# Two of seven block products of an expert layer split once more into seven

## The chip, the cores and the metric

The kernel runs on one core of a Trainium2 chip. The metric is the device time of one execution in microseconds (us). TensorE multiplies, VectorE (DVE) and ScalarE (ACT) work element by element, GpSimd (POOL) and SyncE (SP) mostly start transfers. TensorE writes its results into banks of a small memory (PSUM), from which VectorE and ScalarE read.

## The reference, cut to what matters

The layer is a gated cross attention followed by a mixture of experts. All is float32. The part that the change touches is the experts' first layer:

```python
# x: 4096 tokens of 512 features; 8 experts, the best 2 for each token, at most cap = 640 tokens per expert
buf = jnp.zeros((e, cap, d), x.dtype).at[e_flat, posc].add(jnp.where(keep[:, None], xf[tok], 0.0))
h = jax.nn.gelu(jnp.einsum('ecd,edf->ecf', buf, w1) + b1[:, None, :], approximate=False)   # 512 -> 2048
out = jnp.einsum('ecf,efd->ecd', h, w2) + b2[:, None, :]                                   # 2048 -> 512
```

`h` is needed by the second layer in full; the results are then weighted and added to the tokens' rows.

## The kernel before, in words

Attention, the router and the dispatch of tokens come first. The third stage, from 1591 us of the span to its end, takes the eight experts one after the other. Per expert the tokens' rows arrive in 5 tiles of 128 (`xb`), are transposed by TensorE (L2105) and copied to `bT` (features on partitions, 640 tokens along the columns).

**First layer.** `hidden(e, idx)` makes one of eight feature blocks: 256 features (two halves, `lo` and `hi`, of 128) for 640 tokens (two halves of `HC` = 320), summed over 512 features of `bT` (two halves of 256, that is two chunks of 128 each). This product of 2 x 2 by 2 x 2 blocks is done with seven instead of eight block products (Strassen's scheme in Winograd's form). Its operands are the blocks and their sums: `w1_forms` of the weights, made by four VectorE sums for each block (`w1_sums`, L1654 to L1657), and `XS` of the tokens, made once per expert (`x_forms`, L2074 to L2077). Each of the seven products is two matmuls of 320 columns; all matmuls pass through the helper `mm` at L2029. Four results share partial sums: ScalarE copies a finished bank into the next one, and further products are added on top. In the order of TensorE:

- product 0 into bank X; ScalarE copies X to Y (L2210; L2207 where the first expert has it early);
- product 3 into Q; ScalarE copies Q to `p5` (L2213);
- product 4 onto Y; ScalarE copies Y to Z (L2216);
- product 1 onto X, and ScalarE's gelu of it (L2221) gives `lo[:, :HC]`;
- product 5 onto Z; ScalarE copies Z to W (L2223); VectorE adds Z and `p5` (L2224) for `hi[:, HC:]`;
- product 6 onto Y; VectorE adds Y and `p5` (L2226) for `lo[:, HC:]`;
- product 2 onto W for `hi[:, :HC]`.

The last three gelus of a block (`owed`, L2229 to L2231) run among the next block's ScalarE operations. Blocks 0 to 3 use the first half of the weights `w1`, blocks 4 to 7 the second. For blocks 0 to 3 of the first expert, products 0 and 1 were already made by `early_product` while rows came in.

**Second layer.** `plain` (two of seven outer products, by matmuls of 256 columns), `deep` (the other five, `7`, `6`, `5`, `4` and `3`, each split into seven products of 128 columns) and `rest` follow. Their operands are formed by VectorE: `left` (L2244 to L2247), `right` (L2259 to L2262), and the inner sums (L2275 to L2284), which lie in `sets[0]` and `sets[1]`. `coefs` (L2093 to L2096) takes weights and indices out of the rows.

**What sets the order.** The order is written by hand. `dv`, `ac`, `ld` and `mm` chain every operation behind the one before of its kind, so each engine works its queue strictly in the order in which the code calls it; the framework adds the waits between engines that the buffers need. The loop over `idx` calls `hidden` and, after it, hands VectorE what later steps need: `w1_sums` for blocks ahead (blocks 4 to 7 after blocks 1 to 4, the next expert's after 6 and 7), `left`, `right`, and the bias rows:

```python
if more and idx == KQ - 1:
    ld(lambda: load_w1(e + 1, 0))
if 1 <= idx <= 4:
    dv(*w1_sums(e, 1, idx - 1))
if idx in (2, 4, 6):
    dv(left(1, idx - 2, idx), left(3, idx - 2, idx))
```

The row tile buffers `xb` are four; the fifth tile of the next expert is loaded (L2040, SP's queue) once VectorE's `coefs` has read the first, and is transposed after the product `6`.

Of the kernel before, what the change touches and what calls it, by code (L numbers as in the profile page):

```python
# [6 lines left out]
F32 = mybir.dt.float32  # L7
I32 = mybir.dt.int32
AF = mybir.ActivationFunctionType
ALU = mybir.AluOpType  # L10
# [4 lines left out]
P = 128  # L15
# [5 lines left out]
def gated_layer(ctx, tc, x, x_t, ctxt, ctxt_t, ctxt_c, ctxt_r, g_xattn, g_ffn, w_sim, w_sim_r, b_sim, W_qv, W_qv_t, b_qv, b_qv_c, w_router, b_router, w1, b1, w2, b2, out):  # L21
# [6 lines left out]
    nc = tc.nc  # L28
    N, D = x.shape
    L = ctxt.shape[0]  # L30
    E, _, FF = w1.shape
    NT = N // P
    DC = D // P
    NF = FF // P
# [76 lines left out]
    with ExitStack() as s1:  # L111
# [6 lines left out]
        ps_tr = s1.enter_context(tc.tile_pool(name="ps_tr", bufs=2, space=PSUM))  # L118
        tt, ts, stt = nc.vector.tensor_tensor, nc.vector.tensor_scalar, nc.vector.scalar_tensor_tensor
# [193 lines left out]
        left = {}  # L313
# [1306 lines left out]
    KH = FH // P  # L1620
    KQ = KH // 2
    KF = 2 * KQ

    def load_w1(e, h):
        w1_of[e, h] = wpool.tile([P, DC, FH], F32, name=f"w1_{e}_{h}", tag="w1", bufs=2)
        return nc.sync.dma_start(w1_of[e, h], w1[e, :, h * FH : (h + 1) * FH].rearrange("(c p) f -> p c f", p=P))
# [15 lines left out]
    def w1_forms(e, h):  # L1642

        W = w1_of[e, h]
        A11, A12, A21, A22 = (W[:, c : c + 2, f * P * KQ : (f + 1) * P * KQ] for f in (0, 1) for c in (0, 2))
        return A11, A12, A22, w1s[0], w1s[1], A21, w1s[2]

    def w1_sums(e, h, f=None):

        cols = slice(None) if f is None else slice(f * P, (f + 1) * P)  # L1650
        A11, A12, A22, S1, S2, A21, S4 = (a[:, :, cols] for a in w1_forms(e, h))
        tt = nc.vector.tensor_tensor
        return [
            lambda: tt(S1, A21, A22, ALU.add),  # L1654
            lambda: tt(S2, S1, A11, ALU.subtract),
            lambda: tt(A21, A11, A21, ALU.subtract),
            lambda: tt(S4, A12, S2, ALU.subtract),  # L1657
        ]
# [3 lines left out]
    with ExitStack() as s2:  # L1662
# [49 lines left out]
        second = c2.tile([P, E], F32, name="second")  # L1712
# [8 lines left out]
        for n in sizes:  # L1721
            t = STEPS[-1][-1] + 1 if STEPS else 0
# [3 lines left out]
        tt, ts, red = nc.vector.tensor_tensor, nc.vector.tensor_scalar, nc.vector.tensor_reduce  # L1726
# [215 lines left out]
        for g in range(len(STEPS)):  # L1942
# [4 lines left out]
            for i in range(ahead):  # L1947
                mm = tile_mm(s, i)
# [16 lines left out]
            if s.n == 2:  # L1965
                with tc.issue_after(mm.ins):
                    place_prev()
                mm = prev.counted
            if s.next is None:

                s.first = ps_mm.tile([P, 2, 512], F32, name="first", tag="mm")[:, 0, :E]
                with tc.issue_after(mm.ins):
                    mm = nc.tensor.matmul(s.first, ones, s.base[:, 0, :], start=True, stop=True)
            elif g + 2 == len(STEPS):

                cnt = ps_mm.tile([P, 2, 512], F32, name="cnt", tag="mm")[:, 0, :E]
                with tc.issue_after(mm.ins):
                    mm = nc.tensor.matmul(cnt, ones, s.base[:, 0, :], start=True, stop=True)
# [19 lines left out]
    with ExitStack() as s3:  # L1998
# [3 lines left out]
        ps_tr = s3.enter_context(tc.tile_pool(name="ps_tr3", bufs=2, space=PSUM, reuse_waits="tile"))  # L2002
        HC = CAP // 2
        MH = 2 * P
        DH = D // 2
        tt, stt = nc.vector.tensor_tensor, nc.vector.scalar_tensor_tensor
        assert KQ == 4 and NST == 5 and DH == 2 * P and KF == 2 * KQ

        banks = [ps_m.tile([P, 512], F32, name=f"bank3_{i}", tag=f"b{i}") for i in range(6)]
        tail = {}  # L2010

        def chained(eng, *ops):

            for op in ops:
                with tc.issue_after(tail[eng].ins) if eng in tail else ExitStack():
                    tail[eng] = op()
            return tail.get(eng)

        def dv(*ops):
            return chained("dv", *ops)  # L2020

        def ac(*ops):
            return chained("ac", *ops)

        def ld(*ops):
            return chained("ld", *ops)

        def mm(ps, a, b, start, stop):
            return chained("pe", lambda: nc.tensor.matmul(ps, a, b, start=start, stop=stop, skip_group_check=True))  # L2029
# [4 lines left out]
        def rows_in(e, s):  # L2034

            if (e, s) == (0, NST - 1):
                xb_of[e, s] = SX.rearrange("p k t -> p (k t)")[:, :R]
            else:
                xb_of[e, s] = sb.tile([P, R], F32, name=f"xb{e}_{s}", tag="xb", bufs=NST - 1)
            return nc.sync.dma_start(xb_of[e, s], buf_d[e * CAP + s * P : e * CAP + (s + 1) * P, :])  # L2040

        sets = [None, None]
# [7 lines left out]
        hT = cb.tile([P, 2, KF, CAP], F32, name="hT", tag="hT")  # L2050
        bT = cb.tile([P, DC, CAP], F32, name="bT", tag="bT")
        B11, B12, B21, B22 = (bT[:, r : r + 2, c : c + HC] for r in (0, 2) for c in (0, HC))
        XT = cb.tile([P, KF, DH], F32, name="XT", tag="XT")
        flat = XT.rearrange("p k d -> p (k d)")
        xT = [flat[:, i * 2 * HC : (i + 1) * 2 * HC].rearrange("p (k t) -> p k t", k=2) for i in range(3)]
        accs = []
        for i in range(NST):
            a = cb.tile([P, D], F32, name=f"acc{i}", tag=f"acc{i}")
            nc.gpsimd.memset(a, 0.0)
            accs.append(a)  # L2060
        b1_t = cb.tile([P, E * NF], F32, name="b1_t", tag="b1")
# [4 lines left out]
        u2, p7 = (cb.tile([P, 2, DH], F32, name=k, tag=k) for k in ("u2", "p7"))  # L2066
# [42 lines left out]
        early = {}  # L2109
# [78 lines left out]

        stored, owed = [], []

        def hidden(e, idx):

            h, f = divmod(idx, KQ)
            col = e * NF + h * KH + f
            lo, hi = hT[:, 0, idx, :], hT[:, 1, idx, :]
            b_lo, b_hi = b1_t[:, col : col + 1], b1_t[:, col + KQ : col + KQ + 1]
            A = [[a[:, k, f * P : (f + 1) * P] for k in range(2)] for a in w1_forms(e, h)]
            X, Q, Y, Z, W = (banks[i][:, :HC] for i in (0, 1, 2 + idx % 2, 4, 5))
            p5 = p5s[idx % 2]
            there = e == 0 and f in early and h == 0  # L2200

            def product(ps, k, start=False):
                for i in range(2):
                    mm(ps, A[k][i], XS[{2: 6, 6: 2}.get(k, k)][i], start and i == 0, i == 1)

            if there:
                ac(lambda: nc.scalar.copy(Y, early.pop(f)))  # L2207
            else:
                product(X, 0, True)
                ac(lambda: nc.scalar.copy(Y, X))  # L2210
            product(Q, 3, True)
            ac(*owed[:1])
            ac(lambda: nc.scalar.copy(p5, Q))  # L2213
            ac(*owed[1:2])
            product(Y, 4)
            ac(lambda: nc.scalar.copy(Z, Y))  # L2216
            ac(*owed[2:])
            owed.clear()
            if not there:
                product(X, 1)  # L2220
                ac(lambda: nc.scalar.activation(lo[:, :HC], X, AF.Gelu, bias=b_lo))  # L2221
            product(Z, 5)
            ac(lambda: nc.scalar.copy(W, Z))  # L2223
            dv(lambda: tt(hi[:, HC:], Z, p5, ALU.add))  # L2224
            product(Y, 6)
            dv(lambda: tt(lo[:, HC:], Y, p5, ALU.add))  # L2226
            product(W, 2)
            owed.extend([
                lambda: nc.scalar.activation(hi[:, HC:], hi[:, HC:], AF.Gelu, bias=b_hi),  # L2229
                lambda: nc.scalar.activation(lo[:, HC:], lo[:, HC:], AF.Gelu, bias=b_lo),  # L2230
                lambda: nc.scalar.activation(hi[:, :HC], W, AF.Gelu, bias=b_hi),  # L2231
            ])


        lo, hi = hT[:, 0], hT[:, 1]
# [4 lines left out]
        def left(kind, k0, k1):  # L2240

            a11, a21, a12, a22, sx = (a[:, k0:k1, :] for a in (A11, A21, A12, A22, SX))
            return {
                1: lambda: tt(sx, a21, a22, ALU.add),  # L2244
                3: lambda: tt(a21, a11, a21, ALU.subtract),
                2: lambda: tt(a11, sx, a11, ALU.subtract),
                4: lambda: tt(a12, a12, a11, ALU.subtract),  # L2247
            }[kind]
# [73 lines left out]
        for e in range(E):  # L2322
            more = e + 1 < E
# [17 lines left out]
            def add(s, c, src):  # L2341
                return lambda: stt(accs[s][:, c], src, cf[:, s : s + 1], accs[s][:, c], ALU.mult, ALU.add)  # L2342

            (B11w, B12w, B21w, B22w), right, inner = output(e)
            bias = [add(s, slice(None), b2_t) for s in range(NST)]
            for idx in range(2 * KQ):
                if more and idx == 2:
                    ld(*[lambda s=s: rows_in(e + 1, s) for s in range(NST - 1)])
                hidden(e, idx)
                if more and idx == KQ - 1:  # L2350
                    ld(lambda: load_w1(e + 1, 0))
                if 1 <= idx <= 4:
                    dv(*w1_sums(e, 1, idx - 1))
                if idx in (2, 4, 6):
                    dv(left(1, idx - 2, idx), left(3, idx - 2, idx))
                if idx == 3:
                    dv(right(1, 0, 4))
                if idx == 5:
                    dv(right(1, 4, 8), *bias[:2])
                if idx == 6:  # L2360
                    dv(*bias[2:])
                    if more:
                        dv(*w1_sums(e + 1, 0, 0), *w1_sums(e + 1, 0, 1))
                if idx == 7 and more:
                    dv(*w1_sums(e + 1, 0, 2))
# [56 lines left out]
            X, Q, Y, Z, W = deep(f7, 3)  # L2422
# [8 lines left out]
            for m in range(2):  # L2431
                dst = accs[2 + m].rearrange("p (j d) -> p j d", j=2)
# [10 lines left out]
            f4, s4, t4 = inner("4")  # L2443
# [87 lines left out]
```

## Time and profile before

| what | value |
|---|---|
| median of 3 runs | 2563.72 us (2563.48 to 2563.97) |
| profiled execution | 2565.51 us, span 2563.7 us |
| granted TensorE clock | 0.998 |
| TensorE matmul busy | 2543.1 us, 99% of the span |
| VectorE busy | 1844.5 us, 72% |
| ScalarE busy | 693.2 us, 27% |
| one expert, transposes to transposes (1774.98 to 1896.49) | 121.51 us; TensorE busy 121.51, VectorE 83.01, ScalarE 36.39 |

The span runs from the first to the last instruction of the profiled execution. A line of a timeline has the start in us, the length, the engine, the source line, the operation, what is written and read, the count, and in brackets how long the engine stood idle before and what released it. Matmuls overlap, and their ends are modelled.

### The profile page before, as it was taken

How to read it: one execution, taken by the hardware profiler on the slowest of the kernel's cores; microseconds unless marked ns; L12 is line 12 of the kernel's file. 1: busy time of each engine (PE TensorE's matmuls, PEld its weight loads, DVE VectorE, ACT ScalarE, POOL GpSimd, SP SyncE). 2: the span in 40 equal slices, each digit the busy share in tenths (PEclk: the TensorE clock that was granted, in tenths of full speed). 3: DMA queues.
4: the chain of work that ended last, by engine and by line, in shares of the span. 5: the costliest groups of instructions: out<-in, count | busy, mean ns of one | idle time of the engine just before them, and what ended most of it. 6: DMA issues, size and time to landing. Idle time of an engine off the chain costs nothing.

```text
span 2563.7 us, 36624 instructions
## 1 busy us (share of the span) xinstructions
PE 2543.1 (99%) x13964; PEld 2196.9 (86%) x13964; DVE 1844.5 (72%) x3670; ACT 693.2 (27%) x1459; POOL 275.9 (11%) x400
## 2 busy tenths in 40 slices
PE   9999999999999999999999999999999999999999
PEld 7788888998988989989989886787888878787978
DVE  8887965977877868759668666767675858484937
ACT  1112302223123123132230244323233232313140
POOL 0101220001001001000000066010101010101010
PEclk9999999999999999999999999999999999999999
DMA  7568795875976857759758795231314141414120
GB/s 260 197 214 299 270 346 168 288 255 177 315 232 207 284 192 263 258 180 304 244 166 281 274 350 202 83 128 66 132 67 156 46 160 38 161 42 156 50 99 21
DMA packets 198399, 488.99 MB, mean 191 GB/s; under 512 B 22462, under 2 KB 79102, under 8 KB 196176
## 3 DMA queue, kind: packets, MB, share of 16 engines
q1 hardware_dynamic: 151984, 386.37, 44.7%
q0 software_dynamic: 21696, 59.07, 6.4%
q10 hardware_dynamic: 24544, 41.21, 4.4%
q8 instruction: 110, 1.80, 0.3%
q14 instruction: 65, 0.53, 0.1%
HBM read 397.40 MB, written 97.52 MB: 193 GB/s over the span
## 4 chain that ended last, share of the span: by engine, by line
PE 88%; issue 5%; DVE 5%; POOL 1%; DMA 1%; ACT 0%; POOLq 0%; SPq 0%; another core or an unknown queue 0%; DVEq 0%; ACTq 0%
PE bank L2029 31%; PE bank L763 21%; PE bank L986 13%; PE bank L1155 6%; PE bank L1512 5%; PE x1p L1757 3%; PE bank L1256 2%; PE p7d L1512 1%; PE p4d L1512 1%; PE bank L815 1%; PE v L1256 1%; DVE SM L1025 1%; PE bank L992 1%; DVE hqT L1192 1%; PE bps L2105 1%
## 5 line engine op out<-in xcount | busy, mean ns | idle before, releaser
L763 PE MATMUL bank<-Qp,kt 128*128 128x256 f32 x1344 | 305.2, 379 | 0.0
L763 PEld LDWEIGHTS bank<-Qp,kt 128*128 128x128 f32 x1344 | 254.4, 190 | 34.1
L2029 PE MATMUL bank<-w,hT 128*128 128x256 f32 (+1 forms) x1280 | 260.7, 359 | 0.7 <-ACT u L2408 0.7
L2029 PEld LDWEIGHTS bank<-w,hT 128*128 128x128 f32 x1280 | 223.8, 190 | 27.4 <-ACT u L2408 1.1
L763 PE MATMUL bank<-q,kt 128*128 128x256 f32 x1008 | 231.3, 379 | 0.0
L2029 PE MATMUL bank<-bT,w 128*128 128x320 f32 x736 | 218.8, 433 | 2.0 <-ACT bank L2216 1.6
L763 PEld LDWEIGHTS bank<-q,kt 128*128 128x128 f32 x1008 | 191.5, 190 | 26.0
L2224 DVE TENSOR_TENSOR hT<-bank,l 128x320 f32<-128x320 f32 x64 | 31.5, 492 | 253.4 <-ACT bank L2223 253.4
L986 PE MATMUL bank<-dt,vf 128*128 128x128 f32 x1680 | 204.8, 275 | 0.0
L986 PEld LDWEIGHTS bank<-dt,vf 128*128 128x128 f32 x1680 | 196.0, 192 | 0.0
L2029 PEld LDWEIGHTS bank<-bT,w 128*128 128x128 f32 x736 | 139.0, 190 | 60.6 <-ACT bank L2216 3.1
L2029 PE MATMUL bank<-XT,w1s 128*128 128x320 f32 x512 | 148.4, 433 | 0.0
L806 DVE TENSOR_TENSOR M<-M,E_all 128x1024 f32<-128x1024 f32 x80 | 97.8, 1223 | 47.8 <-ACT E_all L723 46.4
L2029 PEld LDWEIGHTS bank<-XT,w1s 128*128 128x128 f32 x512 | 97.2, 190 | 40.6 <-ACT bank L2207 0.4
L2397 POOL DMA_INDIRECT out<-acc,ti x40 | 39.6, 990 | 819.2 <-DVE acc L2342 812.5
L1757 PE MATMUL x1p<-W,q2T 128*128 128x264 f32 x512 | 119.8, 396 | 0.5 <-DVE p1d L1527 0.5
L1757 PEld LDWEIGHTS x1p<-W,q2T 128*128 128x128 f32 x512 | 98.8, 195 | 18.0 <-DVE p1d L1527 0.9
L719 DVE TENSOR_TENSOR E_all<-bank,p5s 128x512 f32<-128x512 f32 x42 | 28.9, 689 | 114.5 <-ACT bank L718 114.5
L893 DVE TENSOR_TENSOR E_all<-E_all,mb 128x1024 f32<-128x1024 f32 x84 | 101.2, 1211 | 10.3 <-ACT mb L868 10.3
L986 PE MATMUL bank<-E_all,vf 128*128 128x128 f32 x828 | 106.5, 275 | 0.0
L894 ACT ACTIVATE E_all<-E_all 128x1024 f32<-128x1024 f32 x84 | 88.8, 1057 | 49.8 <-DVE E_all L893 49.3
L986 PEld LDWEIGHTS bank<-E_all,vf 128*128 128x128 f32 x828 | 99.8, 192 | 0.3
(602 smaller groups left out, 4755.9 us busy)
## 6 DMA issues: line engine op xcount, KB each, us to landing
vf<-vf_d SPq DMA_DIRECT2D x122, 768.0 KB
kt<-kt_d SPq DMA_DIRECT2D x84, 512.0 KB
w<-in_w SPq DMA_DIRECT2D x16, 2048.0 KB
w<-in_w SPq DMA_DIRECT2D x32, 1024.0 KB
kt<-in_ctxt_t SPq DMA_DIRECT2D x84, 384.0 KB
wp<-wt_d SPq DMA_DIRECT2D x56, 520.0 KB
buf_d<-zero SPq DMA_DIRECT2D x80, 129.0 KB
xb<-buf_d SPq DMA_DIRECT2D x39, 258.0 KB
```

The lines of the kernel that those rows point to most:

```text
L763: nc.tensor.matmul(ps[:, jl, :], kts[j][:, KSLOT[p], k, :], B[p][:, k, :], start=start and jl == 0 and k == 0, stop=stop and k == 1, skip_ ...
L806: tt(M, M, e[:, :, h], ALU.max)
L893: live[g]["last"] = tt(e, e, m, ALU.subtract)
L894: live[g]["exp"] = nc.scalar.activation(e, e, AF.Exp)
L986: nc.tensor.matmul(ps, a[:, j, :], rhs[r][:, j, :], start=start and j == 0, stop=j == NP - 1 and (rest is None or add is None), skip_group ...
L1155: nc.tensor.matmul(ps[b], vt[:, j - i * JH, b * P : (b + 1) * P], right(j) if j < NJ else right_c, start=start and j == 0 and b == 0, stop ...
L1256: mm = nc.tensor.matmul(acc[k][:, b, :], a[:, b * P : (b + 1) * P], r, start=start and b == 0, stop=stop, skip_group_check=True,)
L1512: nc.tensor.matmul(ps[m], A[p][:, k, m * P : (m + 1) * P], wt[:, k, :], start=start and k == 0, stop=stop and k == DC - 1, skip_group_chec ...
L1757: mm = nc.tensor.matmul(ps[:, j, :B1], qTs[g][:, c, q * P : (q + 1) * P], W1[:, c, j, :], start=(c == 0), stop=(c == DC - 1))
L2029: return chained("pe", lambda: nc.tensor.matmul(ps, a, b, start=start, stop=stop, skip_group_check=True))
L2224: dv(lambda: tt(hi[:, HC:], Z, p5, ALU.add))
L2397: sc = nc.gpsimd.indirect_dma_start(out=out[:, :], out_offset=rows_of(ti, s), in_=accs[s][:, :], in_offset=None, bounds_check=N - 1, oob_i ...
```

## The change

In blocks 0 to 5, products 6 and 2 are taken out of `hidden`. For each pair of neighbouring blocks (0 and 1, 2 and 3, 4 and 5) the two blocks' products 6 are one product of 256 features, 320 tokens and 256 summed features. It is split into halves in all three and made by seven matmuls of 160 columns; the same for product 2. Such a small set, `parts(e, k, pair, ...)`, is woven into a following block in three steps (`first`, `second`, `third`): set "6" of a pair into block 1, 3 or 5, set "2" into block 2, 4 or 6. Its partial sums X, W and Q lie in one bank of the transposes' pool, Y and Z in another bank. VectorE adds the results onto `hT` (four adds a set), and ScalarE's gelus follow. `deep_x` and `deep_w` form the small sets' operands on VectorE, partly in place, partly in `sets[1]`. Blocks 6 and 7 keep all seven products. The `left` pairs and the load of the next expert's first weights move to later blocks.

```diff
+        def deep_x(k):
+            b, (t1, t2, t4, t3) = x_of[k]
+            b11, b12, b21, b22 = (b[:, c, d : d + HH] for c in range(2) for d in (0, HH))
+            return [
+                lambda: tt(t1, b12, b11, ALU.subtract),
+                lambda: tt(t2, b22, t1, ALU.subtract),
+                lambda: tt(t3, b22, b12, ALU.subtract),
+                lambda: tt(t4, b21, t2, ALU.subtract),
+            ]
+
+        def deep_w(e, k, pair):
...
+            return [
+                lambda: tt(s1, a21, a22, ALU.add),
+                lambda: tt(s2, s1, a11, ALU.subtract),
+                lambda: tt(a21, a11, a21, ALU.subtract),
+                lambda: tt(s4, a12, s2, ALU.subtract),
+            ]
+
+        def parts(e, k, pair, c_bank):
+            XWQ = ps_tr.tile([P, DC, P], F32, name=f"d{e}_{k}{pair}", tag="tr").rearrange("p c t -> p (c t)")
+            X, W, Q = (XWQ[:, i * HH : (i + 1) * HH] for i in range(3))
+            YZ = banks[c_bank][:, : 2 * HH]
+            Y, Z = YZ[:, :HH], YZ[:, HH:]
...
+            def first():
+                mm(X, a11, b11, True, True)
+                ac(lambda: nc.scalar.copy(Y, X))
+                mm(Q, s1, t1, False, True)
+                mm(W, a22, t4, False, True)
+
+            def second():
+                mm(Y, s2, t2, False, True)
+                ac(lambda: nc.scalar.copy(Z, Y))
+                mm(X, a12, b21, False, True)
+
+            def third():
+                mm(Z, s3, t3, False, True)
+                mm(Y, s4, b22, False, True)
+
+            adds = [
+                lambda: tt(dst[:, :, HH:], dst[:, :, HH:], Q.unsqueeze(1).to_broadcast([P, 2, HH]), ALU.add),
+                lambda: tt(dst[:, :, :HH], dst[:, :, :HH], XWQ[:, : 2 * HH].rearrange("p (f t) -> p f t", f=2), ALU.add),
+                lambda: tt(dst[:, 0, HH:], dst[:, 0, HH:], Y, ALU.add),
+                lambda: tt(... Z.unsqueeze(1).to_broadcast([P, 2, HH]), ALU.add),
+            ]
...
         def hidden(e, idx):
...
-            product(Q, 3, True)
-            ac(*owed[:1])
-            ac(lambda: nc.scalar.copy(p5, Q))
-            ac(*owed[1:2])
-            product(Y, 4)
-            ac(lambda: nc.scalar.copy(Z, Y))
-            ac(*owed[2:])
-            owed.clear()
+            if there and idx:
+                ac(lambda: nc.scalar.copy(Y, early.pop(f)))
+                step(0)
+                product(Y, 4)
+                due(1)
+                ac(lambda: nc.scalar.copy(Z, Y))
+                step(1)
+                product(Q, 3, True)
+                ac(lambda: nc.scalar.copy(p5, Q))
+                step(2)
+                due(1)
+            else:
...
+                step(0)
+                due(1)
+                product(Q, 3, True)
+                ac(lambda: nc.scalar.copy(p5, Q))
+                step(1)
...
+                product(Y, 4)
+                ac(lambda: nc.scalar.copy(Z, Y))
+                step(2)
+                due(1)
             if not there:
                 product(X, 1)
                 ac(lambda: nc.scalar.activation(lo[:, :HC], X, AF.Gelu, bias=b_lo))
+            due(len(owed))
+            if split:
+                dv(lambda: tt(lo[:, HC:], Y, p5, ALU.add))
             product(Z, 5)
-            ac(lambda: nc.scalar.copy(W, Z))
+            if part:
+                dv(*part[3])
...
+            ac(lambda: nc.scalar.copy(hi[:, :HC] if split else W, Z))
             dv(lambda: tt(hi[:, HC:], Z, p5, ALU.add))
-            product(Y, 6)
-            dv(lambda: tt(lo[:, HC:], Y, p5, ALU.add))
-            product(W, 2)
+            if not split:
+                product(Y, 6)
+                dv(lambda: tt(lo[:, HC:], Y, p5, ALU.add))
+                product(W, 2)
...
                 hidden(e, idx)
-                if more and idx == KQ - 1:
+                if more and idx == KQ:
                     ld(lambda: load_w1(e + 1, 0))
                 if 1 <= idx <= 4:
                     dv(*w1_sums(e, 1, idx - 1))
-                if idx in (2, 4, 6):
-                    dv(left(1, idx - 2, idx), left(3, idx - 2, idx))
+                if idx == 0:
+                    dv(*deep_w(e, "6", 0), *deep_x("6"), *deep_w(e, "2", 0), *deep_x("2"))
+                if idx == 1:
+                    dv(*deep_w(e, "6", 1), *deep_w(e, "2", 1))
+                if idx == 4:
+                    dv(*deep_w(e, "6", 2), *deep_w(e, "2", 2))
+                if idx in (4, 6, 7):
+                    k = (0, 2, 4)[(4, 6, 7).index(idx)]
+                    dv(left(1, k, k + 2), left(3, k, k + 2))
```

More of the change, by code (lines that the diff above doesn't have):

```diff
@@ L2189, in gated_layer, with w_of @@
         stored, owed = [], []
+        DEEP_IDX = 6
+        HH = HC // 2
+        flat_set = [t.rearrange("p a b -> p (a b)") for t in sets[1]]
+        x_of = {
+            k: (b, [flat_set[i][:, q * HH : (q + 1) * HH] for q in range(3)] + [p7[:, i - 5, :HH]])
+            for k, i, b in (("2", 5, xT[2]), ("6", 6, B22))
+        }
+        def w_of(k, pair):
+            n = 3 * (2 * (pair % 2) + (k == "6"))
+            return [flat_set[2 + (n + q) // 4][:, (n + q) % 4 * P : ((n + q) % 4 + 1) * P] for q in range(3)]
@@ new lines, in deep_x @@
+        def deep_x(k):
[8 more added lines that the diff above has]
+        def deep_w(e, k, pair):
+            a = w1_forms(e, pair // 2)[int(k)]
+            f = pair % 2 * 2 * P
+            a11, a12, a21, a22 = (a[:, c, f + r : f + r + P] for r in (0, P) for c in range(2))
+            s1, s2, s4 = w_of(k, pair)
+            return [
[4 more added lines that the diff above has]
+            ]
@@ new lines, in parts @@
+        def parts(e, k, pair, c_bank):
[3 more added lines that the diff above has]
+            Y, Z = YZ[:, :HH], YZ[:, HH:]
+            a = w1_forms(e, pair // 2)[int(k)]
+            f = pair % 2 * 2 * P
+            a11, a12, s3, a22 = (a[:, c, f + r : f + r + P] for r in (0, P) for c in range(2))
+            s1, s2, s4 = w_of(k, pair)
+            b, (t1, t2, t4, t3) = x_of[k]
+            b11, _, b21, b22 = (b[:, c, d : d + HH] for c in range(2) for d in (0, HH))
+            dst = hT[:, 0, 2 * pair : 2 * pair + 2, HC:] if k == "6" else hT[:, 1, 2 * pair : 2 * pair + 2, :HC]
+            def first():
[14 more added lines that the diff above has]
+                lambda: tt(dst[:, 0, HH:], dst[:, 0, HH:], Y, ALU.add),
+                lambda: tt(
+                    dst[:, 1, :].rearrange("p (d t) -> p d t", d=2), dst[:, 1, :].rearrange("p (d t) -> p d t", d=2),
+                    Z.unsqueeze(1).to_broadcast([P, 2, HH]), ALU.add,
+                ),
+            ]
+            return first, second, third, adds, dst
@@ L2195, in hidden @@
             lo, hi = hT[:, 0, idx, :], hT[:, 1, idx, :]
-            b_lo, b_hi = b1_t[:, col : col + 1], b1_t[:, col + KQ : col + KQ + 1]
+            bias_of = lambda i, n: (lambda c: b1_t[:, c : c + 1])(e * NF + i // KQ * KH + i % KQ + n * KQ)
+            b_lo, b_hi = bias_of(idx, 0), bias_of(idx, 1)
             A = [[a[:, k, f * P : (f + 1) * P] for k in range(2)] for a in w1_forms(e, h)]
@@ L2200, in hidden @@
             there = e == 0 and f in early and h == 0
+            split = idx < DEEP_IDX
+            part = None
+            if 1 <= idx <= DEEP_IDX:
+                k, pair = ("6", idx // 2) if idx % 2 else ("2", idx // 2 - 1)
+                part = parts(e, k, pair, 5 if split else 2 + (idx + 1) % 2)
             def product(ps, k, start=False):
@@ L2204, in product, with step, due @@
                     mm(ps, A[k][i], XS[{2: 6, 6: 2}.get(k, k)][i], start and i == 0, i == 1)
-            if there:
-                ac(lambda: nc.scalar.copy(Y, early.pop(f)))
-            else:
-                product(X, 0, True)
-                ac(lambda: nc.scalar.copy(Y, X))
-            product(Q, 3, True)
-            ac(*owed[:1])
-            ac(lambda: nc.scalar.copy(p5, Q))
-            ac(*owed[1:2])
-            product(Y, 4)
-            ac(lambda: nc.scalar.copy(Z, Y))
-            ac(*owed[2:])
-            owed.clear()
+            def step(i):
+                if part:
+                    part[i]()
+            def due(n):
+                ac(*owed[:n])
+                del owed[:n]
+            if there and idx:
+                ac(lambda: nc.scalar.copy(Y, early.pop(f)))
+                step(0)
[7 more added lines that the diff above has]
+                due(1)
+            else:
+                if there:
+                    ac(lambda: nc.scalar.copy(Y, early.pop(f)))
+                else:
+                    product(X, 0, True)
+                    ac(lambda: nc.scalar.copy(Y, X))
+                step(0)
[3 more added lines that the diff above has]
+                step(1)
+                if not part:
+                    due(1)
+                product(Y, 4)
+                ac(lambda: nc.scalar.copy(Z, Y))
+                step(2)
+                due(1)
             if not there:
@@ L2221, in hidden @@
                 ac(lambda: nc.scalar.activation(lo[:, :HC], X, AF.Gelu, bias=b_lo))
+            due(len(owed))
+            if split:
+                dv(lambda: tt(lo[:, HC:], Y, p5, ALU.add))
             product(Z, 5)
-            ac(lambda: nc.scalar.copy(W, Z))
-            dv(lambda: tt(hi[:, HC:], Z, p5, ALU.add))
-            product(Y, 6)
-            dv(lambda: tt(lo[:, HC:], Y, p5, ALU.add))
-            product(W, 2)
[L2228 to L2232, printed above, removed]
+            if part:
+                dv(*part[3])
+                n = int(k == "2")
+                for i in range(2):
+                    owed.append(
+                        lambda d=part[4][:, i, :], b=bias_of(2 * pair + i, n): nc.scalar.activation(d, d, AF.Gelu, bias=b)
+                    )
+            ac(lambda: nc.scalar.copy(hi[:, :HC] if split else W, Z))
+            dv(lambda: tt(hi[:, HC:], Z, p5, ALU.add))
+            owed.insert(0, lambda: nc.scalar.activation(hi[:, HC:], hi[:, HC:], AF.Gelu, bias=b_hi))
+            if not split:
+                product(Y, 6)
+                dv(lambda: tt(lo[:, HC:], Y, p5, ALU.add))
+                product(W, 2)
+                owed.extend([
+                    lambda: nc.scalar.activation(lo[:, HC:], lo[:, HC:], AF.Gelu, bias=b_lo),
+                    lambda: nc.scalar.activation(hi[:, :HC], W, AF.Gelu, bias=b_hi),
+                ])
         lo, hi = hT[:, 0], hT[:, 1]
```

## The prediction

> **What bounds the kernel now.** I read the page's busy shares, then the chain of waits in order of time, then the timelines of single engines. About 0.2% (5.1 us) is what a measurement of this kernel can tell from no change.
>
> First the busy shares, then seven pieces of the chain (start, length, what) for one expert:
>
> ```profile
> PE 2543.1 (99%) x13964; PEld 2196.9 (86%) x13964; DVE 1844.5 (72%) x3670; ACT 693.2 (27%) x1459; POOL 275.9 (11%) x400
> ```
>
> ```profile
> 1803.55 92.94 PE bank L2029 x456
> 1896.49 0.87 PE bps L2105 x8
> 1897.37 6.98 PE bank L2029 x32
> 1904.35 0.87 PE bps L2105 x8
> 1905.22 19.41 PE bank L2029 x144
> 1924.63 0.44 PE bps L2105 x4
> 1925.07 92.92 PE bank L2029 x456
> ```
>
> TensorE is the chain: one expert follows the next every 121.51 us (1774.98 to 1896.49) without a gap. So a TensorE column saved is time saved, and any new TensorE wait is time lost. The pieces give the pitch of one half of an f32 matmul (each is recorded as two). 32 halves of 256 columns take 6.98: 0.2181 each. 19.41 holds 32 of them and 112 of 128 columns: 0.1110. 92.94 holds 64, 168 and 224 of 320 columns: (92.94 - 13.96 - 18.65)/224 = 0.2693.
>
> **Removed and added on TensorE.** Two products of two blocks were 8 halves of 320 columns, 8 x 0.2693 = 2.154. They become 14 halves of 160. No row has 160; between 128 and 256 columns it is 0.1378 (ends: half of 0.2693 = 0.1347; 160/128 of 0.1110 = 0.1388), so 1.929. Saved: 0.225 per small set (0.21 to 0.27), 6 sets per expert, 8 experts: **-10.8 us** (-10.1 to -12.9).
>
> **Wait A, inside every small set.** `first()` puts X, W and Q of a set into one PSUM bank. It multiplies X, has ScalarE copy X to Y, and goes on to Q. In the built (not run) order of the changed kernel the Q matmul carries a wait on ScalarE, and the next writes to Y and X carry none, so the wait is on that copy. The profile already shows two users of one bank taking turns: VectorE L2224 reads bank Z 0.04 after ScalarE L2223 has read it. Its price, from the first expert, where TensorE has nothing between a product and the copy it needs:
>
> ```profile
> 1594.46 1.34 PE L2029 MATMUL bank<-bT,w 128*128 128x320 f32 x4 [0.55 <-ACT bank L2216]
> ...
> 1600.14 0.41 ACT L2216 COPY bank<-bank 128x320 f32<-128x320 f32 x1 [0.19 <-PE bank L2029]
> ...
> 1600.61 1.34 PE L2029 MATMUL bank<-bT,w 128*128 128x320 f32 x4 [0.50 <-issue]
> ```
>
> Start to start is 6.15 for 20 halves worth 5.39: an uncovered copy costs 0.76. The first four after the wait take 1.34, not 1.24 as later fours do: a restart costs 0.10. So Y's last half ended at 1594.46 + 0.10 + 5.39 = 1599.95, the copy began 0.19 later, and TensorE restarted 0.06 after it. Now the set: count from the end of the big product X0. ScalarE first copies X0 (from 0.19; its next operation follows 0.32 on, at 0.51). X ends at 0.275, is ready at 0.465, is copied from 0.51. A 160-column copy, between the rows of 128 (250 ns) and 320 (410), is 0.277: done 0.79, restart at 0.85, plus 0.10. Without the wait Q would start at 0.275: **0.68 lost** (0.53 if ScalarE does not hold it up and no restart is paid, 0.85 if another operation stands ahead). Everything else of the block is queued behind it. Blocks 2, 3, 4 and 6 pay this: 4 x 8 x 0.68 = **+21.8**. Blocks 1 and 5 wait longer for VectorE, which covers it.
>
> The Trainium skill, "PSUM — Partial Sum Buffer", section on bank collisions, says that semaphores must guard PSUM by bank and quadrant, not by address, a disjoint column range included; that speaks against X and Q in one bank. By addresses alone there would be no wait A and the sum would be 21.8 lower; by the rule it stands. No run shown yet has a TensorE write beside a ScalarE read of other columns.
>
> **Waits B and C, for VectorE's forms.** VectorE's queue at the end of a block:
>
> ```profile
> 1842.75 0.49 DVE L2224 TENSOR_TENSOR hT<-bank,l 128x320 f32<-128x320 f32 x1 [6.46 <-ACT bank L2223]
> 1843.33 0.49 DVE L2226 TENSOR_TENSOR hT<-bank,l 128x320 f32<-128x320 f32 x1
> 1843.74 0.41 DVE L1654 TENSOR_TENSOR w1s<-w 128x256 f32<-128x256 f32 x1
> 1844.19 0.42 DVE L1655 TENSOR_TENSOR w1s<-w1s,w 128x256 f32<-128x256 f32 x1
> 1844.53 0.42 DVE L1656 TENSOR_TENSOR w<-w 128x256 f32<-128x256 f32 x1
> 1844.87 0.42 DVE L1657 TENSOR_TENSOR w1s<-w,w1s 128x256 f32<-128x256 f32 x1
> ```
>
> An add of 320 columns holds VectorE 0.41; 256 columns hold it 0.34, or 0.45 where the next needs its result. Durations 416 ns (256) and 683 (512) give 1.04 ns a column, so 128 columns hold it 0.20 (0.31 dependent, 0.28 to the result) and 160 columns 0.24 (0.345, 0.317).
>
> B: block 0 now ends with product Z, five products after its start, and the `hi` add waits for Z, then for ScalarE's copy of that bank: E + 0.19 + 0.45 = E + 0.64 (E: TensorE's end of block 0). Only then does the queue reach `deep_w`, `deep_x` of set "6": s1 starts at E + 1.05, t1 at 1.97, ready 2.29; t4 ready at 3.11. TensorE wants s1, t1 at E + 1.077 + 0.275 = 1.35 and gets them at 2.35: 1.00 + 0.10. Then W needs t4: TensorE is free at 2.73, t4 seen at 3.17: 0.44 + 0.10. Together 1.65.
>
> C: block 5 wants s1 of pair 2, which stands after block 4: `hi` add at E + 0.67, its 0.41, four `w1_sums` 1.46, s1 from 2.54, seen at 2.88 instead of 1.35: 1.53 + 0.10 = 1.63. In both, the block's products queue behind. The other sets are formed at least a block ahead. B and C: 8 x 3.28 = **+26.2** (1.3 to 2.1 each: 20.8 to 33.6).
>
> **Wait D, the rows of the last tile.** VectorE runs without a gap from 1888.55 to 1921.2 and then frees the buffer for the load that feeds the transposes at 1924.5:
>
> ```profile
> 1921.25 0.34 SPq L2040 DMA_DIRECT2D xb<-buf_d  x1
> ...
> 1924.47 0.60 PE L2105 MATMUL bps<-ident,xb 128*128 128x128 f32 x4
> ...
> 2290.01 0.63 PE L2105 MATMUL bps<-ident,xb 128*128 128x128 f32 x4 [0.88 <-DMA xb<-buf_d]
> ```
>
> That load's traffic ends about 2.4 after its issue in six experts; in the seventh it took 4.1 and TensorE did wait (last line). Moving the `left` pairs (from after blocks 2, 4, 6 to after 4, 6, 7) puts one more pair, 1.44, into this run. Counted from the end of the last block (1896.49 - 6.98 = 1889.51), the issue moves from 31.74 to 33.18, the rows are seen near 35.7, and TensorE wants them at 34.96: 0.7 + 0.10, seven times: **+5.6** (0 to 9, if the run starts earlier or VectorE comes late to it).
>
> **Hidden at no cost.** VectorE's added work, 24 operations of 0.20, 8 of 0.24 and 6 times 1.46 of adds (three of 0.41, one of 0.24), is 15.5 us per expert, beside 38.5 idle (83.0 of 121.5 busy); where it is not hidden it shows as B, C, D. The four adds of a set end before the next block's ScalarE copy needs their bank (about 0.5 before the block ends, and the copy comes 1.5 after), so ScalarE does not wait for them. ScalarE itself gets 12 small copies per expert and is 27% busy. The load of the next expert's first weights is issued one block later, some 8 us: now issued at 1859.5, its traffic is over by 1868 and VectorE first reads it at 1884.7, so 17 are spare; the other half, behind it in SP's queue, is issued near 1890 in any case. If that cover went, VectorE's wait would add to D.
>
> **First expert.** For its blocks 1 to 3 the change puts a product between the copy of Y and its use, so three of its 0.76 waits go (-2.3). But no X0 runs ahead of their sets: B begins 1.08 sooner and costs that more, and in A ScalarE still has two copies ahead (free at 0.86 instead of 0.51), 0.35 more in two blocks. Together **-0.5** (-2 to +1).
>
> **Sum.** -10.8 + 21.8 + 26.2 + 5.6 - 0.5 = +42.3. The profiled execution took 2565.51 with a span of 2563.7; the median of the runs is 2563.72, and the sum is set on that: 2606. All low ends together: +23; all high: +61.
>
> **Rivals.**
> 1. The saving arrives and the waits hide (faster): the copy and the forms land before TensorE asks, 2553. It decides only if an expert's new waits stay under 10.8/8 = 1.35 us; B alone is 1.65 by rows. Chance 0.03, with 0.02 for a balance within 5 us.
> 2. Wait A is cheap (another write lets Q pass early): 2606 - 21.8 = 2584. Against: the wait in the built order. Chance 0.07. That the change does not make its small sets at all is excluded by that order, which has them.
> 3. VectorE falls behind: by my count it has only 0.15 us to spare before block 7's `hi` add. If 2 us more pile up, D grows by 2 x 7 = 14: 2620. For it: the gapless run of 32 us; against: gaps after 1921. Chance 0.13.
> 4. My case, 2606: 0.75.
>
> The range 2590 to 2620 leaves out the faster case, most of rival 2 and the top of rival 3. Slower by over 0.2%: 0.95.
>
> **What would show it.** TensorE idle of 0.5 to 0.7 released by the new ScalarE copy in four blocks per expert; about 1.5 by VectorE in blocks 1 and 5; an expert's period near 121.5 - 1.35 + 6.0 + 0.8 = 127.0; transposes released by the load. A period under 121, or no idle before Q, proves me wrong; DVE-released idle in the second layer would be rival 3.

## The result, and the profile after

| | before | changed |
|---|---|---|
| median of 5 runs | 2563.48 us (2561.88 to 2563.97) | 2609.74 us (2609.28 to 2610.49) |
| profiled execution, its span | 2565.51, 2563.7 us | 2609.41, 2607.4 us |
| granted TensorE clock | 0.998 | 0.999 |
| one expert, transposes to transposes | 121.51 us | 127.12 to 127.30 us |

The changed kernel is slower: ratio 1.0180, 95% interval 1.0168 to 1.0192. The forecast was 2606 us within 2590 to 2620.

The busy shares of the changed kernel, from the page:

```profile
PE 2544.9 (98%) x14252; PEld 2215.0 (85%) x14252; DVE 1975.6 (76%) x4118; ACT 711.5 (27%) x1555; POOL 275.8 (11%) x400
```

TensorE's busy time has hardly moved (2543.1 before), though columns were saved: at every wait the record of the last matmul runs past its pitch, and the first one after it takes longer (0.16 and 0.11 us at the wait below). The share says little here; the new waits have to be read directly. This is who TensorE waited for in the third stage (engine, line, releaser: us in total, times, longest):

```profile
PE d L2029 <- ACT bank L2244: 13.2, 28, 1.1
PE d L2029 <- DVE l L2222: 11.6, 8, 1.5
PE d L2029 <- ACT hT L2341: 6.6, 7, 0.9
PE bps L2105 <- DMA xb<-buf_d: 5.6, 7, 0.9
PE d L2029 <- DVE l L2209: 2.0, 1, 2.0
PE d L2029 <- DVE l L2212: 1.8, 8, 0.2
PE d L2029 <- ACT bank L2313: 1.3, 3, 0.4
PE d L2029 <- issue: 0.4, 1, 0.4
```

`d` is the bank with X, W and Q of a small set. L2244 is ScalarE's copy of X: wait A. It should come 32 times, in four blocks of eight experts; the other four are the last two lines, where the records name the copy of the big product ahead of it (L2313), or nothing. L2222 is the first operation of `deep_w` (s1): wait C, once per expert. L2209 and L2212 are the first and last of `deep_x` (t1, t4): wait B, in two steps. The line with L2341 is also B: the Q matmul of block 1 waits for ScalarE and VectorE together, and a gelu that stood behind the copy ended last by the records (experiment 1 settles the name). The transposes waited for the load of rows in seven experts: D. Every wait that the prediction named is there, and none that it did not name is over 0.7 us in all.

Wait A in block 2 of one expert, from the timeline:

```profile
1856.06 0.43 PE L2029 MATMUL d<-XT,w 128*128 128x160 f32 x2
1856.26 0.41 ACT L2313 COPY bank<-bank 128x320 f32<-128x320 f32 x1 [0.65 <-PE bank L2029]
...
1856.58 0.28 ACT L2244 COPY bank<-d 128x160 f32<-128x160 f32 x1
...
1856.92 0.54 PE L2029 MATMUL d<-l,l 128*128 128x160 f32 x2 [0.42 <-ACT bank L2244]
```

X is multiplied at 1856.06. ScalarE, still in the copy of the big product (L2313), takes X at 1856.58, and Q starts 0.06 after that copy, at 1856.92. The bracket says 0.42, but the loss is larger. X is recorded as 0.43 long, where two halves at their pitch take 0.27 (0.135 each in experiment 6's chain), so 0.16 without work stands as busy; and the restart costs 0.11 (0.54 for two halves instead of 0.43).

Wait B, from the chain in order of time, at the end of block 0:

```profile
1846.22 0.43 ACT hT L2339
...
1846.67 0.49 DVE hT L2340
1847.17 0.21 DVE l L2222
...
1848.10 0.24 DVE l L2209
...
1848.92 0.25 DVE l L2212
1849.17 0.04 issue
1849.21 0.54 PE d L2029 x2
```

The chain leaves TensorE: ScalarE's copy of Z, the `hi` add (L2340), then `deep_w` and `deep_x` in queue order, and only after t4 does the W matmul start. Q had started in between, on t1 (L2209); its row in the timeline names the gelu instead:

```profile
1848.47 0.51 PE L2029 MATMUL d<-l,l 128*128 128x160 f32 x2 [0.95 <-ACT hT L2341]
```

Wait C, the same view in block 5: the four `w1_sums` (L1654 to L1657) lie between the `hi` add and s1.

```profile
1879.57 0.49 DVE hT L2340
1880.06 0.34 DVE w1s L1654
...
1881.19 0.34 DVE w1s L1657
1881.53 0.21 DVE l L2222
1881.74 0.14 issue
```

Wait D, the load and the transposes that need it (SP's queue and TensorE on the timelines):

```profile
1811.71 0.34 SPq L2040 DMA_DIRECT2D xb<-buf_d  x1
...
1814.42 0.63 PE L2105 MATMUL bps<-ident,xb 128*128 128x128 f32 x4 [0.74 <-DMA xb<-buf_d]
```

From the end of that expert's last block (1785.54 - 6.98 = 1778.56) the issue comes at 33.15; 33.18 was forecast. The transposes start at 35.86, where they were wanted at 34.96.

### The profile page after: what moved, and what is told of

Its sections match the earlier page's. It is cut to its first block, busy times and chain, and to the rows that moved or that the text cites. A ratio compares the mean times of both kernels' runs of the same rounds, so it can differ in the third digit from the quotient of the medians.

```text
span 2607.4 us, 37846 instructions
## 1 busy us (share of the span) xinstructions
PE 2544.9 (98%) x14252; PEld 2215.0 (85%) x14252; DVE 1975.6 (76%) x4118; ACT 711.5 (27%) x1555; POOL 275.8 (11%) x400
## 3 DMA queue, kind: packets, MB, share of 16 engines
q1 hardware_dynamic: 151984, 386.37, 43.9%
## 4 chain that ended last, share of the span: by engine, by line
PE 86%; issue 6%; DVE 5%; DMA 1%; POOL 1%; ACT 1%; POOLq 0%; SPq 0%; another core or an unknown queue 0%; DVEq 0%; ACTq 0%
PE bank L2029 28%; PE bank L763 20%; PE bank L986 12%; PE bank L1155 6%; PE bank L1512 5%; PE x1p L1757 3%; PE bank L1256 2%; PE d L2029 2%; PE p7d L1512 1%; PE p4d L1512 1%; PE bank L815 1%; PE v L1256 1%; DMA xb<-buf_d 1%; POOL buf_d L1906 1%; PE bps L2105 1%
## 5 line engine op out<-in xcount | busy, mean ns | idle before, releaser
L2029 PE MATMUL bank<-bT,w 128*128 128x320 f32 x736 | 211.1, 432 | 0.6 <-ACT bank L2322 0.6
L2029 PE MATMUL bank<-XT,w1s 128*128 128x320 f32 x512 | 156.2, 433 | 0.0
L2029 PEld LDWEIGHTS bank<-l,l 128*128 128x128 f32 x736 | 92.9, 192 | 7.6
```

## The experiments

The experiments were measured in two series. The kernel before took 2557.09 us (median of 9) in that of the first four, and 2565.00 (median of 12) in that of the last two; the changed kernel was run in neither. By the profiles the lead of the first series lies ahead of the third stage: the last transposes before it (L85) start at 1589.4 us in the kernel before and 1589.6 in the changed one, at 1581.0 to 1583.4 in experiments 1 to 4, and at 1591.4 and 1589.2 in 5 and 6. What makes it the runs do not show. So each experiment is judged by its own profile: by one expert's period, transposes to transposes, against the changed kernel's 127.20 (mean of six: from 1658.39 to 2421.60), and by the list of TensorE's waits. The expected totals were written from 2609.74 and lie some 6 us high for the first series.

**1. Another bank for Q and W.**

```diff
-            X, W, Q = (XWQ[:, i * HH : (i + 1) * HH] for i in range(3))
+            QW = ps_tr.tile([P, DC, P], F32, name=f"q{e}_{k}{pair}", tag="tr").rearrange("p c t -> p (c t)")
+            X, Q, W = XWQ[:, :HH], QW[:, :HH], QW[:, HH : 2 * HH]
...
-                mm(Q, s1, t1, False, True)
+                mm(Q, s1, t1, True, True)
...
-                lambda: tt(dst[:, :, :HH], dst[:, :, :HH], XWQ[:, : 2 * HH]...
+                lambda: tt(dst[:, 0, :HH], dst[:, 0, :HH], X, ALU.add),
+                lambda: tt(dst[:, 1, :HH], dst[:, 1, :HH], W, ALU.add),
```

> Q and W of each small set go to a second bank; X keeps its own. Theory (Q waits because ScalarE's copy of X and TensorE's write of Q share a bank): TensorE idles no more for that copy in blocks 2, 3, 4 and 6, 8 x 4 x 0.66 = 21 us less, some 1 us more in the first expert: about 2588 us; the waits in blocks 1 and 5 stay, since they are VectorE's. Rival (the copy is waited for whatever bank Q lies in, or VectorE's added work is the cause): 2610 us, idle before Q as before.

Measured: 2579.38 us (2577.68 to 2579.77), ratio to before 1.0086 (1.0072 to 1.0100); period 124.3. TensorE's four largest waits:

```profile
PE q L2029 <- DVE l L2222: 11.6, 8, 1.5
PE q L2029 <- DVE l L2209: 8.7, 8, 2.0
PE bps L2105 <- DMA xb<-buf_d: 5.6, 7, 1.0
PE q L2029 <- DVE l L2212: 1.9, 8, 0.3
```

The wait on the copy is gone from all blocks, 2.9 us per expert (2.64 expected); C, D and B stay as they were, B now under its own name, L2209. The matmuls, the copy and VectorE's work are the same but for one add split in two, so what made Q wait was that it shared a bank with X. Each such bank is also one tile of the program, and no run parts the two: whether the wait is set by the bank or by the tile stays open.

**2. The first operands ahead of block 0.**

```diff
+                if idx == 0:
+                    dv(*deep_w(e, "6", 0), *deep_x("6"))
                 hidden(e, idx)
...
                 if idx == 0:
-                    dv(*deep_w(e, "6", 0), *deep_x("6"), *deep_w(e, "2", 0), *deep_x("2"))
+                    dv(*deep_w(e, "2", 0), *deep_x("2"))
```

> The operands of set 6 of the first pair are formed ahead of block 0 instead of after it; nothing else moves. Theory (place in VectorE's queue): in block 1 the wait of about 1.65 us on VectorE goes, and the 0.66 on the copy of X shows in its place: 8 x 1.0 = 8 us less and 1 more in the first expert, 2601 us. Rival (the amount of VectorE's added work, not its place): the same work is done, 2609 to 2610 us.

Measured: 2593.54 us (2592.97 to 2594.32), ratio 1.0141 (1.0126 to 1.0157); period 126.1, that is 1.1 less. TensorE's two largest waits:

```profile
PE d L2029 <- ACT bank L2244: 17.9, 39, 1.1
PE d L2029 <- DVE l L2222: 11.6, 8, 1.4
```

Wait B is gone in the seven later experts, and A shows in its place: 39 times, the 32 of the changed kernel and seven in block 1. The same work in another place of the queue, so it was the place.

**3. The third pair's operands one block earlier.**

```diff
+                if idx == 3:
+                    dv(*deep_w(e, "6", 2))
                 if idx == 4:
-                    dv(*deep_w(e, "6", 2), *deep_w(e, "2", 2))
+                    dv(*deep_w(e, "2", 2))
```

> The weight operands of set 6 of the third pair are formed after block 3 instead of after block 4. Theory: in block 5 the wait of about 1.6 us on VectorE becomes the 0.66 on the copy of X, 8 x 0.95 = 7.6 us less: 2602 us. Rival (amount of VectorE's work): 2609 to 2610 us.

Measured: 2594.36 us (2594.05 to 2596.62), ratio 1.0147 (1.0132 to 1.0163); period 126.1, 1.1 less. The wait on L2222 (11.6 us in all) has left the list, and A comes 40 times: the 32 of the changed kernel and eight in block 5.

```profile
PE d L2029 <- ACT bank L2244: 18.3, 40, 1.1
PE d L2029 <- ACT hT L2341: 6.6, 7, 0.9
```

**4. The row operations earlier.**

```diff
+            if more:
+                dv(*coefs(e + 1, (0,)))
             dv(left(4, 0, 8))
...
-                dv(*coefs(e + 1, (0,)))
                 ld(lambda: rows_in(e + 1, NST - 1))
```

> The four small operations that read the first row tile of the next expert stand some 15 us earlier in VectorE's queue, so the load of the fifth tile is issued earlier. Theory (a late issue, 0.8 us in each of seven experts): the transposes wait no more, 5.6 us less: 2604 us. Rival (the load itself has become slower beside other traffic): less than 2 us of change.

Measured: 2595.32 us (2593.58 to 2595.82), ratio 1.0147 (1.0131 to 1.0162); period 126.11, 1.1 less (0.8 expected). No wait for the rows is left in the list. An earlier issue would hide a slower load too, so the rival is settled by the DMA view: the load's traffic ends 2.1 to 2.4 us after its issue in all seven experts of the changed kernel, and 2.2 to 2.4 in six of seven before. The load was late because it was issued late.

**5. Q and W after the big product.**

```diff
             def first():
                 mm(X, a11, b11, True, True)
                 ac(lambda: nc.scalar.copy(Y, X))
-                mm(Q, s1, t1, False, True)
-                mm(W, a22, t4, False, True)
 
             def second():
+                mm(Q, s1, t1, False, True)
+                mm(W, a22, t4, False, True)
```

> Only the order of TensorE changes: Q and W of a small set come after the big product 3 instead of before it, so that product covers ScalarE's copy of X, and VectorE has 1.08 us more for the operands. Theory: no idle for the copy in any block (21 us less), the two waits on VectorE shrink from 1.65 and 1.63 to about 0.55 each (8 x 2.2 = 17 us less): about 2571 us. Rival (VectorE's added work bounds the blocks): at most the 21 us, 2589 us or more.

Measured: 2571.47 us (2570.22 to 2573.89), ratio 1.0024 (1.0014 to 1.0035), in the series where before took 2565.00; period 122.3, 4.9 less (4.8 expected from 8 experts' 38). The waits left in the small sets:

```profile
PE d L2029 <- DVE l L2222: 3.0, 8, 0.4
PE d L2029 <- DVE l L2212: 1.8, 8, 0.2
```

Product 3 lies between X and Q, so the shared bank costs nothing. C is cut by that product's length ((11.6 - 3.0)/8 = 1.08), and of B only the wait for t4 is left. The rival is out: VectorE's work is unchanged.

**6. All four together.** The order of experiment 5, with the edits of 2, 3 and 4.

> The order of e5 together with the operands formed ahead of block 0 and after block 3 and the early row operations. Theory: no new wait is left, so the saving on TensorE shows: 2563.5 - 10.8 - 2.3 (first expert's own waits) - 0.9 (one late load of before) = 2549.5 us, an expert in 120.1 us. Rival (a next wait takes the place of those removed, or 160-column matmuls run slower than their pitch): 2556 us or more, up to 2564.

Measured: 2553.99 us (2553.36 to 2557.37), ratio to before 0.9961 (0.9947 to 0.9974), in the series where before took 2565.00: 11.0 us less, where 14.0 were expected. The period is 120.10 to 120.12 (120.1 expected). All waits of TensorE that the list has for the third stage:

```profile
PE bank L2029 <- ACT bank L2298: 1.7, 3, 0.6
PE bank L2029 <- ACT u L2536: 0.7, 1, 0.7
PE bank L2029 <- ACT bank L2322: 0.6, 1, 0.6
```

L2298 is a copy in the first expert's blocks 1 to 3, where no big product hides it: the order of experiment 5 takes Q and W away from between this copy and its use. This is most of what is missing from the expected total. From its first big product to the next transposes the first expert takes 60.77 (1591.26 to 1652.03) against 62.01 before, 1.24 less, where the terms made 3.65 (6 x 0.225 for the sets and 2.3 for these waits). One expert, busy time of the engines in one stretch, first the changed kernel, then this one:

```profile
1785.54:1912.66 127.12, 122.06 (x691) 102.76 (x689) 99.41 (x224) 38.69 (x100) 10.11 (x10) 1.00 0.28 100
```

```profile
1772.14:1892.26 120.12, 120.12 (x690) 102.54 (x689) 99.32 (x224) 39.14 (x100) 10.11 (x10) 1.00 0.29 106
```

The columns are the stretch, its length, the busy time of PE, PEld, DVE, ACT and POOL (with the number of instructions), then granted clock, DMA share and GB/s. VectorE does the same 99 us in both; in the second TensorE has no gap. So neither the amount of added work nor the small sets themselves made the kernel slower, only the four waits. This version is faster than both kernels, by 0.4% against the one before.

## Why the prediction was right, by its steps

- **The saving.** Forecast 0.225 us a set. Experiment 6 has it clean: (121.51 - 120.11)/6 = 0.23.
- **Wait A**, 0.68 forecast. From one Q matmul to the next, over two blocks that both wait (1856.92 to 1864.89), it is 7.97 us; the same stretch without waits takes 7.28 in experiment 6 (small-set pieces at 1840.28 and 1847.56 of its chain): 0.69.
- **Wait B**, 1.65 forecast. From X of block 1 (1847.09) to X of block 2 (1856.06) it is 8.97: 8.97 - 7.28 = 1.69.
- **Wait C**, 1.63 forecast. From Q of block 4 (1872.87) to Q of block 5 (1881.88) it is 9.01: 1.73. Of the 0.1 more, 0.08 is that TensorE started 0.14 after s1 (the "issue" in the chain above), where 0.06 had been counted.
- **Wait D**, 0.8 forecast. What is left of the period: 127.20 - 121.51 + 1.40 - 4 x 0.69 - 1.69 - 1.73 = 0.91; experiment 4 took away 1.09. The issue came as forecast, but the rows were seen a little later after it (35.86 instead of 35.7).
- **Hidden steps.** The load of weights and the small copies caused no wait. But "ScalarE does not wait for them" holds only from the second expert on. In the first, without X0 ahead, the chain runs through the set's adds before ScalarE may write Y:

```profile
1603.91 0.29 PE d L2029 x2
1604.20 0.30 DVE hT L2260
1604.50 0.41 DVE hT L2261
1604.98 0.29 ACT bank L2244
1605.31 0.81 PE d L2029 x4
```

  So the term for the first expert was mis-sized. From its first big product to the next transposes it took 62.01 (1591.45 to 1653.46) and takes 66.73 (1591.66 to 1658.39): 4.72 more. With the waits and the saving as measured above, 4.78 of that are accounted for (4 x 0.69 + 1.69 + 1.73 - 1.40), so the term was -0.1 and not -0.5, inside its range of -2 to +1.
- **Rival 3.** VectorE did not fall behind. In front of block 7's `hi` add it had 0.52 us to spare, not 0.15:

```profile
1777.27 0.49 DVE L2340 TENSOR_TENSOR hT<-bank,l 128x320 f32<-128x320 f32 x1 [0.52 <-ACT bank L2339]
```

- **The sum.** +42.3 forecast. Between the profiled executions it is 2609.41 - 2565.51 = 43.9, between the medians 46.3. Of the 2.4 between those two, 2.0 come from the kernel before, whose profiled execution lay that far above its median. No large errors cancel: each wait came within 0.3 us of its forecast size, and experiments 1 to 4 took each one away by itself.

The rule of the Trainium skill ("PSUM — Partial Sum Buffer", bank collisions) told which way the sum goes. The trace agrees that the program makes a write wait for a read of other columns of the bank: Q stood 0.42 us behind the copy of X, and with Q in another bank (experiment 1) it did not. What the chip does to a write and a read of one bank without the wait was not tried, since that would be a race.

## What to carry to other kernels

When TensorE is the bound, a smaller product pays only as far as the new hand-overs to other engines are covered by work that TensorE has in front of them. Here the same work took 46 us more or 11 us less than before, by its order alone. For each new matmul ask three things: which engine last touched its bank (any column of it), what stands ahead of its operand in the queue that makes it, and which load waits at the end of that queue.

## What had not been expected

The loss at a wait is larger than the idle that the trace shows: 0.42 idle stood for 0.69 lost, the rest being 0.16 that counts as busy and a restart of 0.11. So the loss of A came as forecast, but the sign that the prediction named for it, idle of 0.5 to 0.7, was set too high. And the kernel before differs by more than some effects here between series: 2557.09, 2563.48 and 2565.00 us (medians), while one expert's period repeats within 0.2 us inside each profile.
